# Two graph layers on one core: the plan of weights, statistics and norms shifted by a stage

## Chip, core and metric

The kernel runs on one core of a Trainium2 chip. The metric is the device time of one execution in microseconds (us), the median of several runs. Engines are named as in the profile: PE is TensorE, with its weight loads in a row of their own (PEld); DVE is VectorE, ACT is ScalarE, POOL is GpSimd, SP is SyncE. DMAs are issued from the queues of SP, ACT and POOL.

## What is computed

```python
# N = 2048 nodes, B = 8 batches, C = 64 channels, D = 16; A = adj (2048 x 2048)
def layer0(x):                       # Chebyshev terms I, A, 2 A A - I
    w = einsum('nd,dkio->nkio', embedding, weight)     # weights of each node
    b = einsum('nd,do->no', embedding, bias)
    x_g = einsum('knm,bmc->bnkc', [I, A, 2 A A - I], x)
    return einsum('bnki,nkio->bno', x_g, w) + b
def layer1(x):                       # the same three terms and a fourth
    apt = softmax(relu(E @ E.T), axis=1)
    ...                              # x_g with [I, A, 2 A A - I, apt]; own weights of each node
x = layernorm(x + layer0(x))
x = layernorm(x + layer1(x))
```

Every node has weights of its own, made from a 16-wide embedding. The product with these weights is the second large work beside the products with A.

## The kernel before

**Stages.** The nodes lie in 8 blocks of 256. A stage (class `Stage`) is one pass over one block; 32 stages stand in the list `stages`. Stages 0 to 7 are layer 0, kk = 0: the product A x (PSUM tile pu, result U). Stages 8 to 15 are layer 0, kk = 1, called half in the code and "(0,1) stages" here: the product A U (PSUM tile pv), with half as many weights. Stages 16 to 23 are layer 1, kk = 0 (pu again, on the new x). Stages 24 to 31 are layer 1, kk = 1: pv, and then a second product of the same size with the softmax.

**Slots.** A stage's large product is a generator (`product_u`, `turned`) that yields after each of its matmuls; the count goes from 0 to 64 (to 128 in stages 24 to 31), by 2 in pu and by 1 in pv. These counts are called slots. All other work is put into slots by `put(stage, slot, function)` and `spread`; when the count passes a slot, its jobs are emitted (`catch_up`). So the order of the instructions on each engine and each queue is written out by hand, and `Pinned` keeps it. A job can stand in the plan of its own stage n or of stage n + 1.

**Jobs.** `weights(g)` makes the node weights: four matmuls (a pw group) of the split embedding with a split pool of weights into a PSUM tile, and a copy into the SBUF tile w. Copies of even g are on DVE and of odd g on ACT; in the (0,1) stages all are on ACT. A stage has 16 such groups, a (0,1) stage 8. w has one buffer. `apply(c)`, four to a stage, multiplies features by node weights (po) and adds the result into acc on DVE, by a mask of 4 rows. `turn` transposes U or x on PE (pt) and copies it into t. `bias` makes pb and, on DVE, bx. `post` writes acc to DRAM (kk = 0), or normalises it in three parts: mean and square, deviation, and scaling with the output. In the (0,1) stages the output is x1, which POOL stores to DRAM and loads back as the tiles X of layer 1. `statistics(s)`, two to a (0,1) stage, computes row maxima and sums of the softmax: scores on PE (pr), copies on DVE, a maximum, low, an exp on ACT, and inv on DVE; it works in the free half of w. `split_weights` loads a raw pool of weights (wraw, and wthird where kk = 0) from the queue of ACT, splits it on DVE into two parts (wsplit), and stores it to DRAM (wd) from POOL. Four splits are made at the start and ten more in stages 1 to 10. wraw, wthird and wsplit have one buffer each.

**Buffers in PSUM.** ps_acc has two buffers of pu or pv. ps_big has two buffers, which pw, po, pt, pb, pr and the scores ps of the last eight stages share in turn.

**Queues.** SP loads the adjacency tiles (a, four buffers, four to a stage), the pools wst, the embeddings e and es (`load_e`), and acc for kk = 1 (`load_acc`); POOL loads acc for kk = 0.

Of the kernel before, what the change touches and what calls it, by code (L numbers as in the profile page):

```python
# [8 lines left out]
F32 = mybir.dt.float32  # L9
F32R = mybir.dt.float32r  # L10
AF = mybir.ActivationFunctionType
ALU = mybir.AluOpType
AX = mybir.AxisListType

P = 128
N = 2048
B = 8
C = 64
# [3 lines left out]
NB = 256  # L22
# [3 lines left out]
GROUPS = NB * B // P  # L26
# [21 lines left out]
def two_graph_layers(ctx: ExitStack, tc: tile.TileContext, x, x_t, adj_b, layers, out):  # L48
# [17 lines left out]
    pe, dve, act, pool = (Pinned(tc, e) for e in (nc.tensor, nc.vector, nc.scalar, nc.gpsimd))  # L66
    sp = Pinned(tc, nc.sync)
# [6 lines left out]
    one = ctx.enter_context(tc.tile_pool(name="one", bufs=1))  # L74
    four = ctx.enter_context(tc.tile_pool(name="four", bufs=4))
    small = ctx.enter_context(tc.tile_pool(name="small", bufs=2))
# [7 lines left out]
    def big(name):  # L84
        return ps_big.tile([P, 2, 512], F32, tag="big", name=name)
# [10 lines left out]
    X = [None] * NJ  # L96
    U = [None] * NJ

    def new_x(j):
        X[j] = feat.tile([P, BC], F32, tag=f"x{j}", name=f"x{j}")  # L100
        return X[j]
# [24 lines left out]
    es = [const.tile([P, NB], F32R, tag=f"es{i}", name=f"es{i}") for i in range(2)]  # L126
    bst = [const.tile([P, C], F32R, tag=f"bst{i}", name=f"bst{i}") for i in range(2)]
    s1 = const.tile([P, N], F32R, tag="s1", name="s1")
# [6 lines left out]
    for li, (e, b) in enumerate(raw):  # L135
# [8 lines left out]
        if li == 1:  # L144
            for q in range(4):
                pool.dma_start(out=s1[q * D:(q + 1) * D, :].bitcast(F32),
                               in_=ed[(q // 2) * D:(q // 2 + 1) * D, :])
# [3 lines left out]
    wd = {k: [dram.tile([P, 8, P], F32, tag=f"wd{k}{c}", name=f"wd{k[0]}{k[1]}{c}") for c in range(v // 8)]  # L151
          for k, v in {(0, 0): V0, (0, 1): V1, (1, 0): V0, (1, 1): V0}.items()}

    def split_weights(li, kk, c):
        part = slice(8 * c, 8 * c + 8)
        a = one.tile([P, 8, P], F32, tag="wraw", name="wraw")
        act.dma_start(out=a, in_=layers[li][1][kk][:, part, :])
        if kk == 0:
            third = one.tile([P, 8, C], F32, tag="wthird", name="wthird")
            act.dma_start(out=third, in_=layers[li][2][:, part, :])  # L160
            dve.tensor_tensor(a[:, :, 0:C], a[:, :, 0:C], third, op=ALU.subtract)
        s = one.tile([P, 8, P], F32R, tag="wsplit", name="wsplit")
        dve.tensor_copy(s, a)
        for r in (32, 96):
            dve.tensor_tensor(s[r:r + 32, :, :], a[r:r + 32, :, :], s[r:r + 32, :, :].bitcast(F32),
                              op=ALU.subtract)
        pool.dma_start(out=wd[li, kk][c], in_=s.bitcast(F32))
# [5 lines left out]
    x1d = [dram.tile([NB * B, C], F32, tag=f"x1d{j}", name=f"x1d{j}") for j in range(NBLK)]  # L173
    cd = [dram.tile([2, SB, P], F32, tag=f"cd{j}", name=f"cd{j}") for j in range(NBLK)]

    def rows_of(t):
        return t.rearrange("(s p) o -> p s o", p=P)

    class Stage:
# [89 lines left out]
                    dve.scalar_tensor_tensor(acc, src, mask[:, i:i + 1], acc, op0=ALU.mult, op1=ALU.add)  # L269


        def post(self, part):
            flat = self.acc.rearrange("p s o -> p (s o)")
            if self.kk == 0:
                if part == 0:
                    pool.dma_start(out=pd[self.li, self.j], in_=flat)
                return
            if part == 0:
                mean = small.tile([P, GROUPS], F32, tag="mean", name="mean")
                dve.tensor_reduce(mean, self.acc, AX.X, ALU.add)  # L280
                dve.tensor_scalar(mean, mean, 1.0 / C, None, op0=ALU.mult)
                dve.tensor_tensor(self.acc, self.acc, mean[:, :, None].to_broadcast([P, GROUPS, C]),
                                  op=ALU.subtract)
                self.sq = one.tile([P, GROUPS, C], F32, tag="sq", name="sq")
                act.activation(self.sq.rearrange("p s o -> p (s o)"), flat, AF.Square)
            elif part == 1:
                dev = small.tile([P, GROUPS], F32, tag="dev", name="dev")
                dve.tensor_reduce(dev, self.sq, AX.X, ALU.add)
                act.activation(dev, dev, AF.Sqrt, bias=eps, scale=1.0 / C)
                self.dev = dev  # L290
            else:
                rstd = small.tile([P, GROUPS], F32, tag="rstd", name="rstd")
                dve.reciprocal(rstd, self.dev)
                dve.tensor_tensor(self.acc, self.acc, rstd[:, :, None].to_broadcast([P, GROUPS, C]), op=ALU.mult)
                if self.li == 1:
                    pool.dma_start(out=rows_of(out[self.j * NB * B:(self.j + 1) * NB * B, :]), in_=self.acc)
                    return
                pool.dma_start(out=rows_of(x1d[self.j]), in_=self.acc)
                nodes = x1d[self.j].rearrange("(n b) o -> n (b o)", b=B)
                for s in range(SB):  # L300
                    pool.dma_start(out=new_x(SB * self.j + s), in_=nodes[s * P:(s + 1) * P, :])
# [83 lines left out]
            self.p[c] = p  # L385


        def statistics(self, s):
            j = SB * self.j + s
            r = self.room[:, s * N:(s + 1) * N]  # L390
            for h in range(2):
                ps = big("pr")
                for i in range(2):
                    at = (2 * h + i) * 512
                    pe.matmul(ps[:, i, :], es[self.j % 2][:, s * P:(s + 1) * P], s1[:, at:at + 512],
                              start=True, stop=True)
                dve.tensor_scalar(r[:, h * 1024:(h + 1) * 1024], ps.rearrange("p a x -> p (a x)"), 0.0, None,
                                  op0=ALU.max)
            dve.tensor_reduce(cst[:, j:j + 1], r, AX.X, ALU.max)
            low = small.tile([P, 1], F32, tag="low", name="low")  # L400
            dve.tensor_scalar(low, cst[:, j:j + 1], -1.0, None, op0=ALU.mult)
            total = small.tile([P, 1], F32, tag="total", name="total")
            act.activation(r, r, AF.Exp, bias=low, accum_out=total)
            dve.reciprocal(inv[:, j:j + 1], total)
# [8 lines left out]
    later = [(0, 1, c) for c in range(V1 // 8)] + [(1, k, c) for k in range(2) for c in range(V0 // 8)]  # L413
    stages = [Stage(n, n // 16, n // 8 % 2, n % 8) for n in range(32)]
    stages[0].load_e()
    for c in range(V0 // 8):
        split_weights(0, 0, c)
    plans = [{} for _ in stages]

    def put(n, i, f, *args):  # L420
        plans[n].setdefault(i, []).append((f, args))

    def spread(n, first, last, jobs):
        for i, job in enumerate(jobs):
            put(n, first + (last - first) * i // max(len(jobs) - 1, 1), *job)

    for n, st in enumerate(stages):
        turned = st.kk == 1
        late = n < 8
        weights = [(st.weights, g) for g in range(st.units // 4)]  # L430
        if late:
            spread(n + 1, 2, 36, weights)
        elif n == 8:
            spread(n, 51, 62, weights)
        elif st.half:
            spread(n, 24, 60, weights)
        else:
            spread(n, 24, 62 if st.kk == 0 else 124, weights)
        at = 38 if late else 12 if turned else 18
        if n + 1 < len(stages):  # L440
            if not turned:
                put(n + 1, 8, st.turn, 1, U)
            for c in range(4):
                put(n + 1, at + c, st.apply, c)
            for k in range(3):
                put(n + 1, at + 6 + 4 * k, st.post, k)
            put(n, 44 if n < 9 else 30, stages[n + 1].load_e)
        if st.kk == 0:
            put(n, 30, st.bias)
            if st.li == 0:  # L450
                put(n, 20, st.load_xt)
            else:
                put(n, 40, st.turn, 0, X)
        put(n, 36, st.load_acc)
        if st.half:
            for s in range(SB):
                put(*((n + 1, 4 + 12 * s) if n == 8 else (n, 30 + 12 * s)), st.statistics, s)
            put(*((n + 1, 20) if n == 8 else (n, 60)), st.store_c)
        if (st.li, st.kk) == (1, 1):
            st.p = [None] * 8  # L460
            for c in range(8):
                put(n, 40 + 8 * c, st.scores, c)
        if 1 <= n <= len(later):
            put(n, 22, split_weights, *later[n - 1])

    for n, st in enumerate(stages):
        done = 0
# [13 lines left out]
        catch_up()  # L481
    for c in range(4):
        stages[-1].apply(c)
    for k in range(3):
        stages[-1].post(k)


# [43 lines left out]
```

## Time and profile before

| | us |
|---|---|
| median of 3 runs | 1817.34 (1814.54 to 1824.83) |
| the profiled execution, own time | 1819.91 |
| its span, first to last instruction | 1818.1 |
| mean granted TensorE clock | 0.967 of full |
| PE busy | 1666.0 |
| DVE busy | 845.8 |
| ACT busy | 464.7 |
| POOL busy | 109.5 |

A row of the profile's timeline gives start, duration, engine, operation, the tiles out<-in, the count of instructions, and in brackets the idle time of the engine before it with what ended it. A row of busy time by stretch gives, after its limits and length, the busy time of PE, PEld, DVE, ACT and POOL with their instructions, the granted clock, the DMA share and GB/s. A pu or pv matmul of the code appears as two instructions.

### The profile page before, as it was taken

To read this page: it belongs to the slowest core of one execution; us is meant where nothing else is said; L and a number is where in the kernel's file an instruction comes from. 1 tells how busy PE (TensorE), PEld (TensorE's weight loads), DVE (VectorE), ACT (ScalarE), POOL (GpSimd) and SP (SyncE) were. 2 spreads that over 40 slices of the span, in tenths; PEclk is the share of its full clock that TensorE was granted. 3 is DMA by queue.
4 is the path that set the end of the run, shared out by engine and by line. 5 is a ranking of instruction groups with operands and counts; after the bars stand their busy time and mean duration, and the time that the engine had idled before them with its cause. 6 is when DMAs were issued, how large, how long until landed. Compare 5 with 4: busy or idle time off the path is not lost.

```text
span 1818.1 us, 26040 instructions
## 1 busy us (share of the span) xinstructions
PE 1666.0 (92%) x11424; PEld 1173.1 (65%) x11424; DVE 845.8 (47%) x1260; ACT 464.7 (26%) x512; POOL 109.5 (6%) x165
## 2 busy tenths in 40 slices
PE   5699888899868989989999999999999999999995
PEld 2355444456656777775555555569888898898884
DVE  2544444444555555555444444443435425434244
ACT  0221112221232333333222222223223132132231
POOL 4000000000010000001000000000000000000000
PEclk8899999999989999999999999999999999999998
DMA  8544445434244443432333444451222222222210
GB/s 282 169 154 147 153 150 171 136 125 146 90 129 132 110 105 113 110 99 84 121 122 126 130 131 129 126 160 70 79 85 75 73 66 87 93 70 79 93 36 12
DMA packets 64112, 207.53 MB, mean 114 GB/s; under 512 B 8928, under 2 KB 13408, under 8 KB 63424
## 3 DMA queue, kind: packets, MB, share of 16 engines
q1 hardware_dynamic: 44256, 145.12, 24.8%
q0 software_dynamic: 14272, 47.12, 8.5%
q10 hardware_dynamic: 5472, 13.63, 2.4%
q8 instruction: 90, 1.47, 0.4%
q14 instruction: 22, 0.18, 0.0%
HBM read 172.24 MB, written 33.57 MB: 113 GB/s over the span
## 4 chain that ended last, share of the span: by engine, by line
PE 68%; DVE 12%; issue 10%; DMA 5%; ACT 5%; POOL 0%; ACTq 0%; POOLq 0%; DVEq 0%
PE pv L42 25%; PE pu L42 20%; PE po L42 11%; PE pw L42 10%; DVE w L42 4%; ACT w L42 3%; DVE acc L42 3%; DVE cst L42 2%; DVE wsplit L42 2%; DMA wthird<-in_w 2%; DMA wraw<-in_w 2%; PE pt L42 1%; DVE t L42 1%; ACT t L42 1%; PE ps L42 1%
## 5 line engine op out<-in xcount | busy, mean ns | idle before, releaser
L42 PE MATMUL pu<-x,a 128*128 128x512 f32 x1024 | 511.2, 616 | 6.0 <-DMA x<-in_x 5.9
L42 PE MATMUL pv<-a,u 128*128 128x256 f32 x2048 | 500.6, 389 | 2.0 <-issue 2.0
L42 PE MATMUL pw<-e,wst 128*128 128x256 f32 x1792 | 418.9, 357 | 46.1 <-DVE w L42 20.5
L42 PEld LDWEIGHTS pv<-a,u 128*128 128x128 f32 x2048 | 381.1, 194 | 69.5 <-issue 24.3
L42 PEld LDWEIGHTS pw<-e,wst 128*128 128x128 f32 x1792 | 279.9, 194 | 192.8 <-issue 99.2
L42 ACT ACTIVATE w<-pw 128x1024 f32<-128x1024 f32 x256 | 258.5, 1020 | 511.9 <-PE pw L42 510.8
L42 DVE COPY w<-pw 128x1024 f32<-128x1024 f32 x192 | 234.2, 1224 | 319.2 <-PE pw L42 314.0
L42 DVE SCALAR_TENSOR_TENSOR acc<-po,mask,acc 128x256 f32<-128x256 f32 (+1 forms) x640 | 252.2, 427 | 164.3 <-PE po L42 154.0
L42 PEld LDWEIGHTS pu<-x,a 128*128 128x128 f32 x1024 | 178.0, 196 | 131.0 <-issue 122.7
L42 PE MATMUL po<-w,t 128*32 128x256 f32 (+1 forms) x5120 | 224.0, 345 | 19.6 <-DVE acc L42 7.8
L42 PE MATMUL pv<-p,x 128*128 128x256 f32 x1024 | 239.4, 379 | 0.0
L42 PEld LDWEIGHTS po<-w,t 128*32 128x32 f32 (+1 forms) x5120 | 123.5, 110 | 130.8 <-issue 69.8
L42 PEld LDWEIGHTS pv<-p,x 128*128 128x128 f32 x1024 | 186.4, 190 | 20.7
L42 DVE SCALAR_TENSOR_TENSOR p<-ps,c 128x512 f32<-128x512 f32 x64 | 44.2, 690 | 108.5 <-PE ps L42 108.5
L42 ACT ACTIVATE sq<-acc 128x1024 f32<-128x1024 f32 x16 | 16.9, 1057 | 276.7 <-DVE acc L42 276.7
L42 ACT ACTIVATE p<-p 128x512 f32<-128x512 f32 x64 | 40.3, 629 | 168.4 <-DVE p L42 168.4
L42 ACT ACTIVATE w<-w,low 128x2048 f32<-128x2048 f32 x16 | 32.0, 2002 | 96.2 <-DVE low L42 96.2
L42 ACT ACT_TABLE_LOAD x32 | 41.1, 1283 | 53.5 <-DMA a<-in_adj_b 52.9
L42 DVE TENSOR_SCALAR t<-pv 64x1024 f32<-64x1024 f32 x16 | 19.6, 1224 | 74.1 <-ACT t L42 74.0
L42 DVE COPY t<-pt 64x512 f32<-64x512 f32 x48 | 33.0, 688 | 39.1 <-PE pt L42 38.7
L42 ACT ACTIVATE t<-pt 64x512 f32<-64x512 f32 x48 | 29.8, 620 | 78.4 <-DVE t L42 78.1
L42 ACT ACTIVATE u<-pu 128x512 f32<-128x512 f32 x16 | 9.6, 597 | 155.0 <-DVE u L42 155.0
(60 smaller groups left out, 574.0 us busy)
## 6 DMA issues: line engine op xcount, KB each, us to landing
a<-in_adj_b SPq DMA_DIRECT2D x128, 512.0 KB, 5.8
wst<-wd SPq DMA_DIRECT2D x112, 512.0 KB, 4.0
bx<-bx POOLq DMA_DIRECT2D x32, 256.0 KB, 3.2
acc<-bx POOLq DMA_DIRECT2D x16, 512.0 KB, 8.0
pd<-acc POOLq DMA_DIRECT2D x16, 512.0 KB, 2.9
acc<-pd SPq DMA_DIRECT2D x16, 512.0 KB, 7.1
wraw<-in_w ACTq DMA_DIRECT2D x14, 512.0 KB, 4.3
wd<-wsplit POOLq DMA_DIRECT2D x14, 512.0 KB, 2.9
```

The lines of the kernel that those rows point to most:

```text
L42: return self._tc.keep_in_program_order(f(*args, **kwargs))
```

## The change

Weights of stages 8 to 15 are made in slots 2 to 18 of the following stage, and those of stages 16 to 23 in slots 2 to 36 of it; before, both were made late in their own stage. A raw pool is loaded a stage before its split (`load_weights`), at slot 10 (at 50 in stage 0), and the split moves from slot 22 to slot 0. The apply of a (0,1) stage stands in two pairs, at slots 20 and 30, its norm at 34, 38 and 42 of the next stage; the statistics stand in the next stage too, each score half in a slot of its own (36, 40, 48, 52) and the rest at 44 and 56. The turn of U moves from slot 8 to 4, the turn of x from 40 to 50, load_acc from 36 to 48 and some load_e from 30 to 44 or 54; stage 0's bias and load_acc move to stage 1. In the last stage the norm is made for each quarter of acc after its apply, with the output on the queue of SP.

```diff
@@ -151,13 +151,21 @@
     wd = {k: [dram.tile([P, 8, P], F32, tag=f"wd{k}{c}", name=f"wd{k[0]}{k[1]}{c}") for c in range(v // 8)]
           for k, v in {(0, 0): V0, (0, 1): V1, (1, 0): V0, (1, 1): V0}.items()}
 
-    def split_weights(li, kk, c):
+    raw_weights = {}
+
+    def load_weights(li, kk, c):
         part = slice(8 * c, 8 * c + 8)
         a = one.tile([P, 8, P], F32, tag="wraw", name="wraw")
         act.dma_start(out=a, in_=layers[li][1][kk][:, part, :])
+        third = None
         if kk == 0:
             third = one.tile([P, 8, C], F32, tag="wthird", name="wthird")
             act.dma_start(out=third, in_=layers[li][2][:, part, :])
+        raw_weights[li, kk, c] = a, third
+
+    def split_weights(li, kk, c):
+        a, third = raw_weights.pop((li, kk, c))
+        if kk == 0:
             dve.tensor_tensor(a[:, :, 0:C], a[:, :, 0:C], third, op=ALU.subtract)
         s = one.tile([P, 8, P], F32R, tag="wsplit", name="wsplit")
         dve.tensor_copy(s, a)
@@ -269,33 +277,35 @@
                     dve.scalar_tensor_tensor(acc, src, mask[:, i:i + 1], acc, op0=ALU.mult, op1=ALU.add)
 
 
-        def post(self, part):
-            flat = self.acc.rearrange("p s o -> p (s o)")
+        def post(self, part, s0=0, s1=GROUPS):
+            a = self.acc[:, s0:s1, :]
+            flat = a.rearrange("p s o -> p (s o)")
+            g = s1 - s0
             if self.kk == 0:
                 if part == 0:
                     pool.dma_start(out=pd[self.li, self.j], in_=flat)
                 return
             if part == 0:
-                mean = small.tile([P, GROUPS], F32, tag="mean", name="mean")
-                dve.tensor_reduce(mean, self.acc, AX.X, ALU.add)
+                mean = small.tile([P, GROUPS], F32, tag="mean", name="mean")[:, 0:g]
+                dve.tensor_reduce(mean, a, AX.X, ALU.add)
                 dve.tensor_scalar(mean, mean, 1.0 / C, None, op0=ALU.mult)
-                dve.tensor_tensor(self.acc, self.acc, mean[:, :, None].to_broadcast([P, GROUPS, C]),
-                                  op=ALU.subtract)
-                self.sq = one.tile([P, GROUPS, C], F32, tag="sq", name="sq")
+                dve.tensor_tensor(a, a, mean[:, :, None].to_broadcast([P, g, C]), op=ALU.subtract)
+                self.sq = one.tile([P, GROUPS, C], F32, tag="sq", name="sq")[:, 0:g, :]
                 act.activation(self.sq.rearrange("p s o -> p (s o)"), flat, AF.Square)
             elif part == 1:
-                dev = small.tile([P, GROUPS], F32, tag="dev", name="dev")
+                dev = small.tile([P, GROUPS], F32, tag="dev", name="dev")[:, 0:g]
                 dve.tensor_reduce(dev, self.sq, AX.X, ALU.add)
                 act.activation(dev, dev, AF.Sqrt, bias=eps, scale=1.0 / C)
                 self.dev = dev
             else:
-                rstd = small.tile([P, GROUPS], F32, tag="rstd", name="rstd")
+                rstd = small.tile([P, GROUPS], F32, tag="rstd", name="rstd")[:, 0:g]
                 dve.reciprocal(rstd, self.dev)
-                dve.tensor_tensor(self.acc, self.acc, rstd[:, :, None].to_broadcast([P, GROUPS, C]), op=ALU.mult)
+                dve.tensor_tensor(a, a, rstd[:, :, None].to_broadcast([P, g, C]), op=ALU.mult)
                 if self.li == 1:
-                    pool.dma_start(out=rows_of(out[self.j * NB * B:(self.j + 1) * NB * B, :]), in_=self.acc)
+                    rows = slice(self.j * NB * B + s0 * P, self.j * NB * B + s1 * P)
+                    sp.dma_start(out=rows_of(out[rows, :]), in_=a)
                     return
-                pool.dma_start(out=rows_of(x1d[self.j]), in_=self.acc)
+                pool.dma_start(out=rows_of(x1d[self.j]), in_=a)
                 nodes = x1d[self.j].rearrange("(n b) o -> n (b o)", b=B)
                 for s in range(SB):
                     pool.dma_start(out=new_x(SB * self.j + s), in_=nodes[s * P:(s + 1) * P, :])
@@ -385,17 +395,18 @@
             self.p[c] = p
 
 
+        def scores_of_rows(self, s, h):
+            ps = big("pr")
+            for i in range(2):
+                at = (2 * h + i) * 512
+                pe.matmul(ps[:, i, :], es[self.j % 2][:, s * P:(s + 1) * P], s1[:, at:at + 512],
+                          start=True, stop=True)
+            dve.tensor_scalar(self.room[:, s * N + h * 1024:s * N + (h + 1) * 1024],
+                              ps.rearrange("p a x -> p (a x)"), 0.0, None, op0=ALU.max)
+
         def statistics(self, s):
             j = SB * self.j + s
             r = self.room[:, s * N:(s + 1) * N]
-            for h in range(2):
-                ps = big("pr")
-                for i in range(2):
-                    at = (2 * h + i) * 512
-                    pe.matmul(ps[:, i, :], es[self.j % 2][:, s * P:(s + 1) * P], s1[:, at:at + 512],
-                              start=True, stop=True)
-                dve.tensor_scalar(r[:, h * 1024:(h + 1) * 1024], ps.rearrange("p a x -> p (a x)"), 0.0, None,
-                                  op0=ALU.max)
             dve.tensor_reduce(cst[:, j:j + 1], r, AX.X, ALU.max)
             low = small.tile([P, 1], F32, tag="low", name="low")
             dve.tensor_scalar(low, cst[:, j:j + 1], -1.0, None, op0=ALU.mult)
@@ -414,6 +425,7 @@
     stages = [Stage(n, n // 16, n // 8 % 2, n % 8) for n in range(32)]
     stages[0].load_e()
     for c in range(V0 // 8):
+        load_weights(0, 0, c)
         split_weights(0, 0, c)
     plans = [{} for _ in stages]
 
@@ -425,43 +437,43 @@
             put(n, first + (last - first) * i // max(len(jobs) - 1, 1), *job)
 
     for n, st in enumerate(stages):
-        turned = st.kk == 1
-        late = n < 8
+        late = n < 24
         weights = [(st.weights, g) for g in range(st.units // 4)]
-        if late:
+        if st.half:
+            spread(n + 1, 2, 18, weights)
+        elif late:
             spread(n + 1, 2, 36, weights)
-        elif n == 8:
-            spread(n, 51, 62, weights)
-        elif st.half:
-            spread(n, 24, 60, weights)
         else:
-            spread(n, 24, 62 if st.kk == 0 else 124, weights)
-        at = 38 if late else 12 if turned else 18
+            spread(n, 50 if n == 24 else 24, 124, weights)
         if n + 1 < len(stages):
-            if not turned:
-                put(n + 1, 8, st.turn, 1, U)
+            if st.kk == 0:
+                put(n + 1, 4, st.turn, 1, U)
+            at = 20 if st.half else 38 if late else 12
             for c in range(4):
-                put(n + 1, at + c, st.apply, c)
+                put(n + 1, at + c + (8 * (c // 2) if st.half else 0), st.apply, c)
             for k in range(3):
-                put(n + 1, at + 6 + 4 * k, st.post, k)
-            put(n, 44 if n < 9 else 30, stages[n + 1].load_e)
+                put(n + 1, at + (14 if st.half else 6) + 4 * k, st.post, k)
+            put(n, 54 if 8 < n < 16 else 44 if n < 25 else 30, stages[n + 1].load_e)
         if st.kk == 0:
-            put(n, 30, st.bias)
+            put(*((n, 30) if n else (1, 1)), st.bias)
             if st.li == 0:
                 put(n, 20, st.load_xt)
             else:
-                put(n, 40, st.turn, 0, X)
-        put(n, 36, st.load_acc)
+                put(n, 50, st.turn, 0, X)
+        put(*((n, 48) if n else (1, 26)), st.load_acc)
         if st.half:
             for s in range(SB):
-                put(*((n + 1, 4 + 12 * s) if n == 8 else (n, 30 + 12 * s)), st.statistics, s)
-            put(*((n + 1, 20) if n == 8 else (n, 60)), st.store_c)
+                for h in range(2):
+                    put(n + 1, 36 + 12 * s + 4 * h, st.scores_of_rows, s, h)
+                put(n + 1, 44 + 12 * s, st.statistics, s)
+            put(n + 1, 62, st.store_c)
         if (st.li, st.kk) == (1, 1):
             st.p = [None] * 8
             for c in range(8):
                 put(n, 40 + 8 * c, st.scores, c)
-        if 1 <= n <= len(later):
-            put(n, 22, split_weights, *later[n - 1])
+        if n < len(later):
+            put(*((n, 10) if n else (n, 50)), load_weights, *later[n])
+            put(n + 1, 0, split_weights, *later[n])
 
     for n, st in enumerate(stages):
         done = 0
@@ -481,8 +493,8 @@
         catch_up()
     for c in range(4):
         stages[-1].apply(c)
-    for k in range(3):
-        stages[-1].post(k)
+        for k in range(3):
+            stages[-1].post(k, 4 * c, 4 * c + 4)
 
 
 def kernel(x, adj, L0_gnn_embedding, L0_gnn_weight, L0_gnn_bias,
```

## Prediction

> **What bounds the kernel now.** I read the page first: TensorE (PE) is busy 92% of the span and makes 68% of the chain that ended last, so only time in which PE stands still, or runs at a reduced clock, can be won.
>
> ```profile
> PE 1666.0 (92%) x11424; PEld 1173.1 (65%) x11424; DVE 845.8 (47%) x1260; ACT 464.7 (26%) x512; POOL 109.5 (6%) x165
> PEclk8899999999989999999999999999999999999998
> PE 68%; DVE 12%; issue 10%; DMA 5%; ACT 5%; POOL 0%; ACTq 0%; POOLq 0%; DVEq 0%
> ```
>
> The reader sees a clock below full in the first half and almost none below it later. So I cut the timeline into the 32 stages (a stage starts where pu or pv restarts). Their lengths: stage 0 45.5 us and stage 1 64.1; 2 to 7 together 310.3; 8 55.2; 9 68.1; 10 to 15 together 282.4 (52.4, 45.4, 47.1, 44.6, 45.7, 47.2); 16 48.5; 17 to 23 46.7 each; 24 73.9; 25 to 31 73.0 each; then 26.3 after the last product. Second view: busy time by stretch, here stage 4's first half, stage 9's first half, stage 13, stage 25.
>
> ```profile
> 217.80:246.50 28.70, 23.46 (x100) 14.71 (x99) 15.66 (x16) 8.00 (x9) 1.56 (x3) 0.94 0.35 119
> 480.90:519.20 38.30, 26.54 (x341) 20.51 (x341) 24.42 (x48) 12.51 (x13) 1.45 (x2) 0.87 0.31 88
> 693.90:738.50 44.60, 40.19 (x425) 32.54 (x424) 26.14 (x50) 17.84 (x18) 3.73 (x5) 1.00 0.38 111
> 1280.70:1353.70 73.00, 73.00 (x465) 61.55 (x465) 30.56 (x40) 18.90 (x22) 1.17 (x1) 1.00 0.26 78
> ```
>
> Stages 25 to 31 have no idle PE; the others do. Third view: the timeline in stage 4 (PE, then DVE) and in stage 9.
>
> ```profile
> 243.34 0.64 PE L42 MATMUL pb<-bst,e 128*128 128x64 f32 x2 [5.24 <-DVE w L42]
> 238.12 0.69 DVE L42 TENSOR_TENSOR wraw<-wraw,wthird 128x512 f32<-128x512 f32 x1 [4.95 <-DMA wthird<-in_w]
> 515.59 2.14 PE L42 MATMUL pr<-s,es 128*128 128x512 f32 x4 [5.79 <-ACT w L42]
> 521.93 0.69 DVE L42 CAST wsplit<-wraw 128x1024 fp32r<-128x1024 f32 x1 [7.95 <-DMA wraw<-in_w]
> 527.84 1.22 PE L42 MATMUL pw<-e,wst 128*128 128x256 f32 x4 [7.34 <-DVE w L42]
> ```
>
> A split on DVE waits for its raw weights, the copies of w behind it wait, both big PSUM buffers stay full, and PE stands. Such waits cost 3.7 to 5.9 us in each of stages 1 to 8 and about 22 us in stage 9.
>
> **The Trainium skill.** "TensorE: Matmul & The Clock Gate", Part 1, "What's actually happening": after an idle window of 3.4 us the array runs at half rate until a busy window has passed. The trace agrees on the effect (0.50 granted from 188.6 to 195.4, around the end of stage 3's 5.2 us wait at 191.1), but a 2.0 us gap at 562.7 was also followed by 0.50 until 567.5; I charge 1.7 us (half of 3.4) for any wait over 2 us. The same page, "Architectural detail", engine queue depths: ACT and DVE are strict FIFO; the rows above agree, a ready copy stands behind a waiting split. "PSUM — Partial Sum Buffer", Specifications: 8 banks of 2 KiB per partition; pu/pv and big take two banks a buffer, two buffers each, so there is no third big buffer.
>
> **The change, part by part.**
>
> *Start (stages 0, 1).* Gone: pb's wait at slot 30 (12.6 us idle at 34.6). But DVE's four splits still end at 63.1, and now a fifth comes ahead of bx, with raw weights whose load ACT can issue only when split 4 has read wraw: 63.1 + 4.3 (median landing) + 0.69 + 2 x 1.22 + bx 2 x 0.68 = 72. The second pw of stage 1 needs pb's buffer, so it starts at 72 in place of 64.5: +7.5. Gone in return: the 3.7 us wait at 89.2, its 1.7 of clock. Sum about **+2**.
>
> *Stages 2 to 7.* Waits before: 30.2 us and 12 us of clock. Now the raw weights are there, but the split stands at slot 0, behind u (ends 0.85 into the stage): 3.9 us with wthird (0.69 + 0.69 + 2.45), 3.2 without. The first copy of w ends at 6.0 or 5.3; the turn of U, moved to slot 4, needs that buffer at 2.6. Waits of 3.4 or 2.7, plus 0.7 (estimate) for the later t copies, plus 1.7 of clock: 33 us in six stages. **-9.** The waits change place rather than vanish.
>
> *Stage 8.* Its own 8 pw groups go to stage 9 (8 x 0.52, the spacing of a group from the timeline); wait 4.3 becomes 2.7. **-5.**
>
> *Stage 9.* It had four statistics; now one pair, no late raw load, one split hidden before the first apply (DVE free at 8.1, apply at 12.8). PE work of a (0,1) stage: pv 128 x 0.216 = 27.65, pw 8 x 0.52, po 4 x 1.1, pr 4 x 0.55: 38.3. 68.1 - 38.6 = **-29.5**.
>
> *Stages 10 to 15.* Same PE work, but from slot 30 on DVE must do, with stage 13's rows: two applies 4.3, mean part 2.7, two score copies and dev between them 3.7, rstd 1.5, first reduce and low 2.5, wait for exp and inv 2.35, two score copies 2.35, reduce and low 2.5, sum 21.8 us; then ACT does exp 2.2, t 2.2, first w copy 1.0: 27.2. It starts 1.2 after slot 30, and PE needs 22.7 from slot 30 to the third pw of the next stage, which needs the buffer of the first. Wait 5.5, clock 1.7: period 45.5 against a mean of 47.1. **-9.5.** The es load now waits for the last pr at slot 52, and the first adjacency tile stands behind it on SP (1.2 issue + 5.8 landing against 5.2 of PE work): about 1.3 us late, hidden under those 5.5, bare if they go.
>
> *Stage 16.* Inherits that wait. The second half of the apply is at slot 30, so the last x1 is normalised at about 41 in place of 22.6; the path from there (trace: 854.0 to 864.1 for POOL store and reload) ends at 51.5, where slot 56 needs X. Before that the fourth pr waits 5 us for the third's copy, behind inv on DVE. 55.5 against 48.5: **+7.**
>
> *Stages 17 to 23.* Weights in slots 2 to 36, as stages 2 to 7 without split: those are 44.7 without their waits, plus a turn of X, 1.1: 45.8 against 46.7. **-6.** *Stage 24* receives stage 23's 16 groups (8.3) and 1.2 where scores meet the applies: **+9.5.** 25 to 31: the same order, nothing. Moved load_acc and load_e on SP and POOL: nothing; they are needed a stage later and land in 2 to 8 us.
>
> *Tail.* Before: mean to product 1804.6 to 1811.55, once; POOL's output then 6.5 to the end. Now four times, each in DVE's order ahead of the next apply: quarter-size 128x1024 steps at about 0.42 (1.22 scaled, with 0.15 fixed; an estimate), square 0.39, sqrt 0.31, rstd 0.25: 3.2 per chunk, so 4 x (2.0 + 3.2) + 0.9 for the table load after 1796.4 ends at 1818; then a 128 KB store on SP, 2.6 by e's 64 KB loads. **+2.5**, bounds -2 and +5.
>
> Sum: 2 - 9 - 5 - 29.5 - 9.5 + 7 - 6 + 9.5 + 2.5 = **-38**. The profiled execution took 1819.9 (span 1818.1), 2.6 over the median and inside the runs' spread; from the median 1817.3 this gives **1780**.
>
> **Bounds of what the trace does not show.** Wait in stages 10 to 16: from none (-7 x 7.2) to 10 us (below). Wait at slot 4 in stages 2 to 8: 0 to 5 us each; taken 2.7 to 3.4 from the rows. The gaps inside po at 562.7, 658.6, 750.5, 795.6 (about 2 us, nothing released them): taken as gone with the applies in pairs; if they stay, up to 8 x 3.7 = 30 us more.
>
> **Rivals.** *A, the (0,1) stages run free.* Were DVE and ACT done with the statistics before the third pw, 7 x 7.2 = 50 us more go: 1730. For it: the work is spread over fewer collisions. Against: the sum of rows, 27.2 against 22.7.
>
> *B, the DVE chain of the statistics becomes the bound; slower.* Place: stages 10 to 16, from the fourth apply's eviction to the second inv on DVE. By my sum that is 21.9 us; the same members took 25.4 in stage 13 (706.98 to 732.42: waits for ACT of 1.18 and 0.40, for PE of 0.33 and 1.53) and 31.9 in stage 10 (563.42 to 595.27, a split among them). Every microsecond over 21.9 is added to the wait at the third pw, seven times. At the middle, 28.6, that is 7 x 6.7 = +47: 1827, slower. It decides from 27.3 on (7 x 5.4 eats the gain). Against: with the apply at slot 30 the pr groups come early, the score copies fill the waits for ACT, and the splits stand before the applies.
>
> *C, the change does not relieve stage 9,* because its waits are of DVE work rather than of raw data (515.6 and 495.3 are of that kind): 1780 + 29.5 = 1809. Against: the statistics of two stages no longer meet there.
>
> **Numbers.** Forecast 0.70, A 0.12, B 0.08, C and similar small gains 0.10. Half a percent (9 us) is about what a measurement of this kernel tells from no change. Faster by more than that 0.86, within it 0.07, slower 0.07. The forecast's errors (six stages of slot-4 waits +-10, seven periods +-14, start, stage 16 and tail +-5 each) give 1760 to 1800; with half of A and C taken in, 1750 to 1812.
>
> **What would show it.** Right: a first wait until about 72 in stage 1; PE waits of 3 us for DVE w at pt in stages 2 to 8, none at pb; stage 9 near 39 us; third pw of stages 10 to 16 waiting 5 to 6 us for ACT w; stage 16 about 7 longer, waiting at pr and X; stage 24 about 83. Wrong: no wait at those pw (A), periods of 50 or more (B), stage 9 over 55 (C), or a new wait of PE for an adjacency tile.

## Result, and the profile after: slower, because of stages 25 to 31

The changed kernel takes 1866.63 us (median of 4 runs, 1865.23 to 1870.68) against 1819.80 for the kernel before in the same comparison: a ratio of 1.0261, 95% interval 1.0225 to 1.0297. It is slower by 2.6%; the forecast was faster by 2%. The profiled execution has a span of 1868.9 us and a mean granted clock of 0.957.

From the page of the changed kernel, the rows that answer to the first three shown of before:

```profile
PE 1662.3 (89%) x11424; PEld 1171.8 (63%) x11424; DVE 847.6 (45%) x1278; ACT 469.1 (25%) x518; POOL 100.4 (5%) x157
PEclk9699999999999999999999999998998989898997
PE 69%; DVE 16%; ACT 5%; issue 4%; DMA 4%; SPq 1%; POOL 0%; DVEq 0%; ACTq 0%; POOLq 0%
```

The clock row has turned round. Before, 8s stood in slices 1, 2 and 12 and, but for the last slice, none later; now the first 27 slices show 9s but for the second, and the last 13 hold five 8s and a 7. The trouble moved to the end. "SPq", SP's queue, is new on the chain.

The same cut into stages, in us, from one profiled execution each, with the repaired kernel of the first experiment below (e1) beside it. Each length runs from a stage's first product instruction to the next stage's:

| stages | before | after | e1 | change, e1 | predicted |
|---|---|---|---|---|---|
| 0, 1 | 109.5 | 116.8 | 114.9 | +5.4 | +2 |
| 2 to 7 | 310.3 | 287.1 | 287.0 | -23.3 | -9 |
| 8 | 55.2 | 47.1 | 47.1 | -8.1 | -5 |
| 9 | 68.0 | 40.1 | 40.5 | -27.5 | -29.5 |
| 10 to 15 | 282.5 | 272.0 | 272.1 | -10.4 | -9.5 |
| 16 | 48.5 | 55.5 | 55.4 | +6.9 | +7 |
| 17 to 23 | 326.9 | 328.7 | 328.6 | +1.7 | -6 |
| 24 | 73.9 | 84.4 | 84.5 | +10.6 | +9.5 |
| 25 to 30 | 437.9 | 518.9 | 437.9 | 0 | 0 |
| 31 and tail | 99.5 | 112.6 | 101.7 | +2.2 | +2.5 |

Until the end of stage 24 the changed kernel is 43 us ahead. It loses 81 us in stages 25 to 30 and 13 in stage 31. Busy time by stretch, changed kernel (columns as in the view of before: limits, length, PE, PEld, DVE, ACT, POOL, granted clock, DMA share, GB/s): stage 4's first half, stage 9, stage 13, stage 25.

```profile
217.90:243.10 25.20, 22.55 (x100) 13.61 (x99) 15.01 (x16) 7.98 (x9) 0.55 (x1) 1.00 0.43 135
456.70:496.80 40.10, 38.96 (x426) 32.48 (x424) 26.32 (x51) 16.02 (x16) 1.72 (x2) 1.00 0.26 78
633.20:677.10 43.90, 39.20 (x424) 32.56 (x424) 25.61 (x50) 18.14 (x18) 3.75 (x5) 1.00 0.31 112
1237.40:1325.00 87.60, 76.16 (x466) 63.59 (x465) 30.56 (x40) 18.90 (x22) 0.00 (x0) 0.92 0.21 65
```

Stage 25 has the same matmuls as before (466 against 465 in the records) and 14.6 us more. Of these PE stands still for 11.44; the other 3.16 are busy time (76.16 against 73.00), the same work at a clock of 0.92.

Which wait is it? The view of waits of the changed kernel, PE's own (us in total, times, longest):

```profile
PE pv L42 <- DMA a<-in_adj_b: 81.0, 13, 11.5
PE pw L42 <- DVE bx L42: 31.7, 1, 31.7
PE pw L42 <- ACT w L42: 23.9, 7, 5.1
```

The product pv waits 81 us for adjacency tiles, a wait that does not stand among the main ones of before. And SP's queue:

```profile
SPq L42 <- DVE acc L42: 327.1, 11, 41.9
```

Eleven times SP stands waiting for DVE to finish acc; eleven is the count of output stores (seven whole stages, four quarters). The timeline in stage 25, which starts at 1237.4: DVE, then SP, then PE.

```profile
1260.56 1.23 DVE L42 TENSOR_TENSOR acc<-acc,rstd 128x1024 f32<-128x1024 f32 x1
1261.82 0.40 SPq L42 DMA_DIRECT2D out<-acc  x1
1262.27 2.38 SPq L42 DMA_DIRECT2D e<-ed  x2
1264.69 0.59 SPq L42 DMA_DIRECT2D c<-cd  x1
1265.33 0.43 SPq L42 DMA_DIRECT2D a<-in_adj_b  x1
1271.97 3.35 PE L42 MATMUL pv<-a,u 128*128 128x256 f32 x7 [11.44 <-DMA a<-in_adj_b]
```

DVE ends the scaling at 1261.79. At 1261.82 SP issues the store, and only then the embeddings, c and the adjacency tile, at 1265.33. PE starts on the tile 6.6 us after that, and had used up the previous one at 1260.5. The store itself takes SP 0.40 us: its row says nothing of the more than 20 us that SP stood in front of it. The Trainium skill ("Perfetto Trace Analysis", "DMA Instruction — HWDGE (DVE, Sync)") says why: the reported start is the moment at which all semaphores are satisfied, and the sequencer is free for the next instruction only after the issue. A wait in front of a DMA is thus invisible in its duration and visible in the queue behind it. The trace agrees: SP issued nothing in this stage before the store, and four issues start within 3.6 us of it.

In the kernel before, POOL issued the store, and SP issued this tile 3.1 us into its stage 25, which starts at 1280.7. Now it is 27.9 us into it.

```profile
1279.09 1.09 SPq L42 DMA_DIRECT2D e<-ed  x2
1283.43 0.33 SPq L42 DMA_DIRECT2D c<-cd  x1
1283.82 0.42 SPq L42 DMA_DIRECT2D a<-in_adj_b  x1
```

Most of this delay is SP's standing, but not quite all: behind the store the embeddings and c take 2.97 us to issue, 1.42 before, and the tile takes 6.6 us from its issue to PE's start, against a median landing of 5.8 us.

### The profile page after: what moved, and what is told of

It reads as the page before. It is cut to its first block, busy times and chain, and to the rows that moved or that the text cites. A ratio compares the mean times of both kernels' runs of the same rounds, so it can differ in the third digit from the quotient of the medians.

```text
span 1868.9 us, 26057 instructions
## 1 busy us (share of the span) xinstructions
PE 1662.3 (89%) x11424; PEld 1171.8 (63%) x11424; DVE 847.6 (45%) x1278; ACT 469.1 (25%) x518; POOL 100.4 (5%) x157
## 4 chain that ended last, share of the span: by engine, by line
PE 69%; DVE 16%; ACT 5%; issue 4%; DMA 4%; SPq 1%; POOL 0%; DVEq 0%; ACTq 0%; POOLq 0%
PE pv L42 27%; PE pu L42 18%; PE po L42 11%; PE pw L42 11%; DVE acc L42 5%; DVE w L42 4%; ACT w L42 3%; DMA a<-in_adj_b 2%; DVE cst L42 2%; ACT t L42 2%; DVE mean L42 1%; DVE t L42 1%; SPq L42 1%; DVE dev L42 1%; PE pt L42 1%
## 5 line engine op out<-in xcount | busy, mean ns | idle before, releaser
L42 PE MATMUL pv<-a,u 128*128 128x256 f32 x2048 | 513.7, 394 | 81.0 <-DMA a<-in_adj_b 81.0
L42 PE MATMUL pu<-x,a 128*128 128x512 f32 x1024 | 500.9, 606 | 5.9 <-DMA x<-in_x 5.9
L42 PE MATMUL pw<-e,wst 128*128 128x256 f32 x1792 | 411.6, 353 | 78.6 <-DVE bx L42 31.7
L42 ACT ACTIVATE sq<-acc 128x1024 f32<-128x1024 f32 (+1 forms) x19 | 17.5, 922 | 284.5 <-DVE acc L42 284.5
L42 DVE COPY u<-pu 128x512 f32<-128x512 f32 x16 | 11.1, 692 | 85.6 <-PE pu L42 85.6
```

Of the source, the lines that this page charges most:

```text
L42: return self._tc.keep_in_program_order(f(*args, **kwargs))
```

## Experiments

Two theories for the 94 us that stages 25 to 31 lose. **Theory 1:** SP issues in order; a store that waits for DVE holds the adjacency tile behind it. **Theory 2:** it is the traffic. On SP the store travels in small packets (in the page of the kernel before, then of the changed kernel), and these slow the loads beside it.

```profile
DMA packets 64112, 207.53 MB, mean 114 GB/s; under 512 B 8928, under 2 KB 13408, under 8 KB 63424
```
```profile
DMA packets 79520, 207.53 MB, mean 111 GB/s; under 512 B 25360, under 2 KB 29840, under 8 KB 78832
```

**e1, the stores back on POOL.**

```diff
-                    sp.dma_start(out=rows_of(out[rows, :]), in_=a)
+                    (pool if g == GROUPS else sp).dma_start(out=rows_of(out[rows, :]), in_=a)
```

> The changed kernel with the whole-stage output stores of layer 1 put back on GpSimd's queue; the last stage's four chunk stores stay on SP. Theory 1 (SP issues in order, so the store that waits for VectorE's scaling holds the adjacency tile behind it): stages 25 to 31 fall from 86 to about 73 us each, 81 + 13 = 94 us less the tail's 4, so 1866 - 90 = about 1777 us, and the wait of the product pv for the adjacency tile (81 us in the changed kernel) is gone. Theory 2 (the store travels over the hardware queue in small packets and slows the loads beside it): the same fall, as the store leaves that queue too. If neither holds, and the stages are long because of the other edits, it stays at about 1866.

Measured: 1777.92 us, 0.9788 of the kernel before (0.9774 to 0.9803). Stages 25 to 30 take 73.0 each, exactly as before. In stage 25 (start 1235.8) SP now issues, by its timeline:

```profile
1238.54 0.33 SPq L42 DMA_DIRECT2D c<-cd  x1
1238.91 0.43 SPq L42 DMA_DIRECT2D a<-in_adj_b  x1
```

The tile goes out 3.1 us into the stage, as in the kernel before. One line of the change thus cost 89 us (1866.63 - 1777.92), and without it the change gains 37.9 (1815.82 - 1777.92). Which of the two theories holds is still open here.

**e2, the kernel before with nothing but that store on SP.**

```diff
-                    pool.dma_start(out=rows_of(out[...]), in_=self.acc)
+                    sp.dma_start(out=rows_of(out[...]), in_=self.acc)
```

> The kernel before with one edit: the output store goes on SP's queue instead of GpSimd's. If the queue of the store alone makes the loss, six stages grow by about 13 us each and the last by some 9 (94 - 4 = 90 in all): 1820 + 90 = about 1910 us under theory 1. Less is possible, since the store stands elsewhere in SP's order here: if no adjacency tile is queued behind it, it stays at 1820. Theory 2 expects 1910 in either case. If the loss needs the other edits (later weights, statistics in bursts), 1820.

Measured: 1907.48 us, 1.0509 (1.0493 to 1.0525): 91.7 us lost. Stages 25 to 30 together take 518.6 (changed kernel: 518.9), and PE's wait is there, once in each of stages 25 to 31:

```profile
PE pv L42 <- DMA a<-in_adj_b: 73.1, 7, 11.7
```

The loss needs none of the other edits.

**e3, the stores on ACT's queue.**

```diff
-                    sp.dma_start(out=rows_of(out[rows, :]), in_=a)
+                    (act if g == GROUPS else sp).dma_start(out=rows_of(out[rows, :]), in_=a)
```

> The changed kernel with the whole-stage output stores issued by ScalarE, a hardware queue like SP's, so with the same packets, but not in front of SP's loads. Theory 1: stages 25 to 31 at about 73 us, 1777 us as with GpSimd, perhaps 1 or 2 us per stage more where ScalarE stands at the store and the next squares come late. Theory 2: the packets are the same, so the stages stay at about 86 us and the time at about 1866.

Measured: 1780.84 us, 0.9807 (0.9792 to 0.9821). Its page shows the packets of the changed kernel, to the last one:

```profile
DMA packets 79520, 207.53 MB, mean 117 GB/s; under 512 B 25360, under 2 KB 29840, under 8 KB 78832
```

The packets are all there and the loss is gone: theory 2 falls as its cause. What is left is 0.3 us a stage (73.3 against 73.0), and ACT's timeline shows the small version of the same wait. ACT is idle for 2.72 us, most of it standing for DVE's scaling, which its row of the store again does not show, and the copy of w behind it comes late (that this copy makes the 0.3 us is not shown):

```profile
1257.22 0.31 ACT L42 ACTIVATE dev<-dev,eps 128x16 f32<-128x16 f32 x1
1259.74 0.41 ACTq L42 DMA_DIRECT2D out<-acc  x1
1260.25 1.02 ACT L42 ACTIVATE w<-pw 128x1024 f32<-128x1024 f32 x1 [2.72 <-DVE acc L42]
```

**e4, the stores on SP, but behind the adjacency loads.** `post` leaves the whole-stage store out, and a job of its own makes it at slot 64 of the next stage.

```diff
+                if self.li == 1 and g == GROUPS:
+                    return
...
+        def output(self):
+            rows = slice(self.j * NB * B, (self.j + 1) * NB * B)
+            sp.dma_start(out=rows_of(out[rows, :]), in_=self.acc)
...
+            if (st.li, st.kk) == (1, 1):
+                put(n + 1, 64, st.output)
```

> The changed kernel with the whole-stage output store still on SP, but put into the order at slot 64 of the next stage, behind the two adjacency loads of slots 32 and 48, when VectorE's scaling is long done. Theory 1: nothing waits behind a waiting store any more, so stages 25 to 31 at about 73 us and 1777 us. Theory 2: same queue, same packets, same bytes: about 1866.

Measured: 1777.82 us, 0.9797 (0.9780 to 0.9813), the same as with POOL. SP in stage 25 (start 1231.0):

```profile
1234.12 0.43 SPq L42 DMA_DIRECT2D a<-in_adj_b  x1
1234.73 0.32 SPq L42 DMA_DIRECT2D acc<-pd  x1
1235.09 0.43 SPq L42 DMA_DIRECT2D a<-in_adj_b  x1
1235.57 0.83 SPq L42 DMA_DIRECT2D wst<-wd  x1
1255.49 0.39 SPq L42 DMA_DIRECT2D out<-acc  x1
1260.61 14.15 SPq L42 DMA_DIRECT2D wst<-wd  x2
```

SP still stands for DVE, until 1255.49 (the scaling ended at 1255.46). But the two tiles are ahead of the store, and nothing behind it is wanted soon. My expectation was off in one word: SP runs ahead of PE, so slot 64 does not mean that the scaling "is long done" when SP gets there. The queue, the bytes and the packets are the same (its page repeats the row shown for e3), and SP still waits for DVE; only the place in the order differs, and the loss is gone. Theory 1 is shown. What the packets add where loads stand directly behind the store, some 1.5 us of issue and under 1 us of landing in stage 25 as estimated from the rows above, no run has separated: in e3 and e4 the loads were out before the store.

The next four kernels stand on e1 and ask how the gain of 38 us comes about.

**e5, the first (0,1) split behind the weight products of stage 1.**

```diff
-            put(*((n, 10) if n else (n, 50)), load_weights, *later[n])
-            put(n + 1, 0, split_weights, *later[n])
+            put(n, {0: 50, 1: 42}.get(n, 10), load_weights, *later[n])
+            put(n + 1, 0 if n else 37, split_weights, *later[n])
```

> On top of e1_out_pool (1778 us): the split of the first (0,1) weights moved from slot 0 of stage 1, where it stands ahead of bx on VectorE, to slot 37, behind the weight products; the load after it moves from slot 10 to slot 42, so that ScalarE does not stand at it. By the prediction's start step PE's 32 us wait for bx ends 8 us earlier (4.3 for the load's landing, 0.7 + 2.4 for the split): 1770 us. Rival: bx is held by another thing than this split (the four first splits, or ScalarE), and the time stays at 1778.

Measured: 1765.45 us, 0.9719 (0.9700 to 0.9739). PE's long wait of stage 1, in the timeline of the changed kernel and of e5:

```profile
74.11 1.20 PE L42 MATMUL pw<-e,wst 128*128 128x256 f32 x4 [31.67 <-DVE bx L42]
```
```profile
64.58 1.20 PE L42 MATMUL pw<-e,wst 128*128 128x256 f32 x4 [21.67 <-DVE bx L42]
```

Against e1, where the wait ended at 72.7, it ends 8.1 us earlier, the 8 expected. Stage 1 is 11.0 us shorter (73.4 against 84.4), since a wait of 2.0 us for wst that ended at 88.9 in e1 went as well.

**e6, the last norm in one piece.**

```diff
         stages[-1].apply(c)
-        for k in range(3):
-            stages[-1].post(k, 4 * c, 4 * c + 4)
+    for k in range(3):
+        stages[-1].post(k)
```

> On top of e1_out_pool: the last stage's norm in one piece after its four applies, and its store on GpSimd, as in the kernel before. Stage 31 with its tail took 101.7 us in e1_out_pool and 99.5 in the kernel before. If the chunks are what costs these 2.2 us, 1776 us; if the chunked norm were a gain that something else hides, slower than 1778.

Measured: 1775.03 us, 0.9774 (0.9759 to 0.9788). The interval overlaps that of e1, but the stage decides: 31 with its tail is 99.5 again against 101.7. The chunks cost 2.2 us, and as much between e8 and e9 below (103.2 and 101.0).

**e7, raw weights fetched together with their split.**

```diff
-            put(*((n, 10) if n else (n, 50)), load_weights, *later[n])
-            put(n + 1, 0, split_weights, *later[n])
+            put(n + 1, 22, load_weights, *later[n])
+            put(n + 1, 22, split_weights, *later[n])
```

> On top of e1_out_pool: raw weights fetched where they are split again (slot 22 of the next stage, load and split together, as in the kernel before); everything else stays. Theory 1 (the load that is late for its split made stages 2 to 8 long): stages 2 to 7 go from 48 back to 52 each and stage 8 from 47 to some 52, +28 together; stage 9, which has only one pair of statistics now, gains a wait of about 6 us: some 1812 us. Theory 2 (stage 9 was long for the raw loads, not for the four statistics): stage 9 returns to 68 as well, some 1834. Theory 3 (the fetch ahead does nothing, moving U's turn and the weights did it): 1778.

Measured: 1806.24 us, 0.9945 (0.9928 to 0.9961), 28 us worse than e1. Stages 2 to 7 take 315.4 in place of 287.0 (before: 310.3), and stage 8 takes 51.1. The old wait is back: DVE, then PE, in e7's stage 4.

```profile
238.70 0.69 DVE L42 TENSOR_TENSOR wraw<-wraw,wthird 128x512 f32<-128x512 f32 x1 [4.74 <-DMA wthird<-in_w]
243.91 0.63 PE L42 MATMUL pb<-bst,e 128*128 128x64 f32 x2 [5.03 <-DVE w L42]
```

So the fetch ahead (with the place of the split) is worth the gain of stages 2 to 8. But stage 9 stays at 38.7: theory 2 of this run falls, and my wait of 6 us did not come either. This does not mean that the raw load cost nothing there before. In the kernel before DVE stood 7.95 us for it in stage 9, and PE 7.34 us behind DVE (rows in the prediction). In e7 the split of stage 9 follows straight on the applies, which end at 499.6, with its raw weights already there. With the statistics and weights moved, a late load does no harm in stage 9; how that stage's 28 us divide among the moves, no run has separated. The start gives 6 us back here, as in e5, because no split stands ahead of bx.

**e8, the bursts undone.** Applies of a (0,1) stage four in a row, each pair of scores with its statistics.

```diff
-                put(n + 1, at + c + (8 * (c // 2) if st.half else 0), st.apply, c)
+                put(n + 1, at + c, st.apply, c)
-                put(n + 1, at + (14 if st.half else 6) + 4 * k, st.post, k)
+                put(n + 1, at + 6 + 4 * k, st.post, k)
-                    put(n + 1, 36 + 12 * s + 4 * h, st.scores_of_rows, s, h)
+                    put(n + 1, 36 + 12 * s, st.scores_of_rows, s, h)
-                put(n + 1, 44 + 12 * s, st.statistics, s)
+                put(n + 1, 36 + 12 * s, st.statistics, s)
```

> On top of e1_out_pool: the applies of the (0,1) stages in one burst again (four in a row at slot 20, the norm's steps from slot 26), and each pair of row scores together with its statistics (slots 36 and 48). If the smaller bursts are worth something, stages 10 to 16 each get 2 to 4 us longer for the evictions that PE then waits for: 14 to 28 in all, 1792 to 1806 us. If only the place (one stage later) matters, 1778. A gain is possible too: without the split of the applies x1 is ready earlier, and stage 16's 7 us of waiting shrink: 1771.

Measured: 1772.77 us, 0.9764 (0.9746 to 0.9783). The interval overlaps that of e1, so a gain is not shown; a loss of 14 to 28 is excluded. By stages it is 2.6 us shorter in 10 to 15, 2.2 in 16, and 1.5 longer in 31 with its tail; but executions that share the code of stages 10 to 15 spread from 266.0 (e4) to 272.2 (e1) there. The smaller bursts are worth nothing here. Nor do they explain why the gaps inside po of the kernel before are gone: with four applies in a row e8 has none in stages 10 to 15 either. PE's waits in e8 no longer list the adjacency tile, for which e1 waits 7.9 us in six stages: the last scores stand at slot 48 instead of 52, so the load of es that waits for them, and the tile behind that load, leave SP sooner (SP waits 118.0 us for these scores, in e1 125.4, over six stages). It is the mechanism of the loss once more, in small.

**e9, the three edits together, and e10, with stage 0's bias later as well.** e9 is e1 with the edits of e5, e6 and e8. e10 adds:

```diff
-            put(*((n, 30) if n else (1, 1)), st.bias)
+            put(*((n, 30) if n else (1, 22)), st.bias)
-        put(*((n, 48) if n else (1, 26)), st.load_acc)
+        put(*((n, 48) if n else (1, 30)), st.load_acc)
```

> The parts that paid, together: stores of layer 1 on GpSimd, the first split behind the weight products, the last norm whole, the (0,1) applies and each pair's scores in one burst. If the savings of the single edits against e1_out_pool (12.5, 2.9 and 5.2 us) lie in different stages and add up: 1778 - 20.6 = about 1757 us. If the 5.2 us of the bursts were spread between runs (its interval touches that of e1_out_pool), 1762.

> As e9_best, and stage 0's bias (pb and bx) moved from slot 1 to slot 22 of stage 1, its load_acc from 26 to 30. PE still stands 22 us in stage 1 until bx has come behind the four first splits on VectorE. If it is the place of bx alone that holds PE, products and the first weights run ahead and some 10 us go: 1747. If the weights behind the same splits hold PE anyway (the later splits' weights come no earlier), the wait only changes its name: within 2 us of e9_best. If the accumulator now comes late for the applies of slot 38, it is slower than e9_best.

Measured: e9 1759.06 us, 0.9673 (0.9655 to 0.9691); e10 1759.14, 0.9673 (0.9654 to 0.9692). The savings add up (e9 is 59.2 us below the kernel before, e1 was 37.9; the difference of 21.3 stands against 20.6 from the three single edits), and e9 beats both kernels. Moving the bias gains nothing: PE's waits, e9 and then e10, show that only the name changed.

```profile
PE pw L42 <- DVE bx L42: 21.3, 1, 21.3
```
```profile
PE pt L42 <- DVE w L42: 22.6, 2, 20.7
```

Some 21 us in stage 1 belong to whatever comes behind the four first splits on DVE, whichever piece that is.

## Why the prediction was wrong, step by step

**The step that failed** is one half-sentence of the sum: "25 to 31: the same order, nothing." The order of the slots is the same there; the queue is not. The diff puts `sp` for `pool` in `post` for the outputs of stages 24 to 31 (the description of the change names SP only for the last), and I priced that only in the tail ("then a 128 KB store on SP"). The seven whole stores were never walked through SP's order, though for stages 10 to 15 the same prediction did it with the load of es and the adjacency tile behind it. The numbers were at hand in the trace of before: the scaling ends some 24 us into a stage, the tile of slot 32 is issued 3 us into it, and 5.8 us pass until it lands. A tile issued after the scaling (24), the store and the loads between (3.5), and landing 5.8 to 6.6 later comes 34 us into the stage, for a product that wants it at 23: 11 us in stage 25, and 3.2 more for the clock. Over the seven stages the waits make 73.8 us (the other 7.2 of the 81.0 lie around the starts of stages 10 to 15, where e1 has 7.9). Stages 25 to 31 are 92 us longer than in e1; the remaining 18 fit the lower clock, as measured for stage 25. e1 to e4 show that the place of the store in SP's order makes the loss. "A new wait of PE for an adjacency tile" stood among the signs of a wrong prediction, but with no mechanism and no price, so the range did not reach it.

**The rest came true in sum, not in every term.** Without that line the change gives -37.9 us by the medians, against the predicted -38. That they agree to a tenth is luck: the stages of the table above add up to -42.5 (the profiled execution of before was slower than its median), and terms off by -14.3 and -3.1 (stages 2 to 7, and 8) stand against others off by +7.7, +3.4 and +2.0 (17 to 23, the start, 9).

- *Stages 2 to 7, -23.3 for -9, and 8, -8.1 for -5.* Predicted were 33 us of waits and clock in six stages; 18.8 came (287.0 less my base of 6 x 44.7). U's turn was charged with the first copy of w, behind the split on DVE. Changed kernel, stage 4, PE and then DVE:

```profile
221.92 1.09 PE L42 MATMUL pt<-ident,u 128*128 128x128 f32 x8 [1.18 <-ACT w L42]
222.67 1.23 DVE L42 COPY w<-pw 128x1024 f32<-128x1024 f32 x1
```

  pt starts before DVE has begun to read the first group, so it doesn't sit in that buffer: it got the one which ACT's copy of the second group frees at 221.87. "Share in turn" was too strict for the two buffers. The wait is 1.2 us instead of 3, and the clock stays at 1.00 (the row of stage 4 above), so the 1.7 us of clock do not come either.
- *Stages 17 to 23, +1.7 for -6.* I took the base of stages 2 to 7 (44.7, their length less the waits) and added 1.1. PE's busy time in stage 18 is 45.6 of 46.7 before and 45.8 of 47.0 after: there was 1.1 us to win in a stage, and a row of busy time for that stage would have said so.
- *Start, +5.4 for +2.* The long wait ended at 72.7 in e1 and at 74.1 in the changed kernel (predicted 72). The wait of pb at 89.2 is gone as entered, but another came near the same place: pw waits 2.0 us (e1) to 2.5 (changed kernel) for wst, which the sum did not have.
- *Stages 9, 16, 24 and the tail* came within 2 us each. For 9 the size is right; that the statistics, and not the raw load, gave it is not shown (e7). Stages 10 to 15 are right in sum, but made differently: in the changed kernel the third pw waits 3.0 to 3.3 us for ACT (predicted 5.5), and the late adjacency tile, 0.9 to 1.5 us (e1: 1.0 to 2.0), is bare instead of hidden. Its 1.3 us was a slip besides: 1.2 + 5.8 - 5.2 is 1.8.

**The rivals.** A needed no wait at the third pw; it is there, 3.0 to 3.3 us in stages 10 to 15 and 5.1 in 16. B needed that wait to be over 5.5; it is smaller, so DVE's chain costs less than the sum gave and not more. C needed stage 9 to stay long; it fell to 40. The kernel ended on the slower side by a mechanism that was none of these.

## What to carry to other kernels

When a DMA moves to another engine's queue, write down what stands behind it there and when its own semaphore comes true: a cheap issue (0.40 us) that waits 20 us delays every load behind it by as much, and its own row does not show it. A store belongs on a queue whose next loads are far off, or behind the loads in the same queue; both cost nothing that shows here (e1 and e4 are equal). For the base of a stage use that stage's own busy time, not that of another kind of stage.

## What the runs showed of the hardware

- The same 512 KB store goes out in packets of 256 B from SP or ACT and in larger ones from POOL: eight stores make 16,384 packets more under 512 B, 2048 each (25312 in e2 less 8928 before). They cost at most 0.3 us a stage in e3 and nothing in e4, where the loads were out before the store; what they cost loads directly behind it is not separated. The store lands in 3.8 us from ACT (e3), 3.8 to 4.0 from SP (e4, e2) and 4.8 from POOL (before), medians.
- Waits of PE of 1.2 us in stage 4 left the granted clock at 1.00; the 11.44 us wait of stage 25 came with 0.92 over the stage. In between it goes both ways in the changed kernel: with waits of 3.32 and 3.02 us near the start of stages 10 and 11 the first half of the stage had a mean of 0.85 and 0.92, with waits of 3.07 and 3.08 us in stages 12 and 13 it had 1.00.
